# Statistics, small products, weights and score rows re-ordered in the front part of a two-layer attention and expert kernel

## The chip, the core and the metric

The kernel runs on one core of a Trainium2 chip. The metric is the device time of one execution in microseconds. The core has five engines with queues of their own: TensorE (PE; weight loads are listed as PEld), VectorE (DVE), ScalarE (ACT), GpSimd (POOL) and SyncE (SP). SP issues nearly all DMAs; GpSimd issues the gathers and scatters by index.

## What is computed

The reference runs two layers on x and a context, both of 8 x 256 tokens of width 256. Cut to what matters here, the first layer is:

```
q, k, v = norm(x) @ Wq + bq, ctx @ Wq + bq, ctx @ Wq + bq          # 16 columns each
corr    = mean over batch and columns of ifft(fft(q) * conj(fft(k)))  # 256 lags
w, lags = top 12 of corr, softmax of them
x       = x + (sum of w * rolled v, repeated 16 times) @ Wout + bout

norm    = layer_norm(layer_norm(x))
scores  = norm @ centroids.T                                   # 2048 tokens, 8 experts
expert e takes the 256 best tokens not yet taken, in the order of e
x       = x + routed tokens + gelu(norm(routed) @ w1[e] + b1[e]) @ w2[e] + b2[e]
```

The second layer is an attention of 16 heads on the context and a mixture of 8 experts (two of them for each token) with a shared expert. It follows the part that is changed and is not touched.

## The kernel before

All engines' queues are written out by hand (`tc.manual_schedule`): the order of the calls in the code is the order of the instructions on each engine. A queue of small closures, `work`, holds products that can be done at any time (keys and values of the second layer, later the experts' products); `fill(us)` takes from it what is to run on TensorE while VectorE works.

The front part, in the order of time:

- The tokens X and the context C are loaded in four pieces each, transposed to `XT` and `CT`, and the tokens' statistics are taken (`stats_x`). `rstd` (lines 1457 to 1477) makes the inverse deviation of a group: a variance, a power of -0.5 on GpSimd, and, as `newton()`, four small instructions that sharpen it. The result `R1` is spread to `rexp`.
- The correlation goes through DRAM (`Gd`, `DG`), then the softmax weights (`Wd`, `CW`).
- `copy_rows(b)` puts a batch of X into PSUM, `spread_rows` adds the attention's output `PB` to it, `take(bs)` (line 1990) takes each tile's statistics on VectorE (with `raw`, only the raw statistics of one instruction, put together later by `put_together` on GpSimd), copies the tile back to X on ScalarE and stores it to `NMd` in DRAM. For one batch, `act_sums` and `squares` do the statistics on ScalarE.
- `factors(q0, q1, eng)` (line 2039) calls `rstd` for tiles q0 to q1, `widen` (2043) spreads the factors `r2` over 32 columns, `factor_rows(k)` (1950) turns them into rows in PSUM (`psr`), and `times_factors` multiplies the raw scores (`ps0` for expert 0, `psx` for all) by them: `n0` and `SC`. `rows_part` adds a term with `cP`, which comes from the small product `pcp`. `means` writes the second column of the factors, `mr2`; both columns lie in `rm`, and `store_factors` (1936) stores them to `NMd`, beside the rows, in four DMAs.
- `SC` is stored to `SCd` in DRAM, and `load_row(e)` (2161) loads the row of expert e, repeated over the partitions. Zeros are stored to `Yd` and `Od`.
- `search(e, ...)` finds the threshold of expert e in five rounds: VectorE counts (`above`, L2198), TensorE sums the counts (`pcn`, L2215), VectorE moves the threshold. For e > 0 the first instruction (`n`, L2190) needs row e.
- `list_tokens(e, ...)` makes the list of tokens and gathers their rows as R (POOL L2323) from `NMd`. `ffn(e, ids, R)` scales R on ScalarE (L2367), transposes it (`prt`, L2387), and runs the two products with the weights of `load_l0(e)` (1812); `Yd` takes the result by a scatter. The lists of one expert and the products of another run beside the searches.

Tiles come from pools. A pool that is opened after another was closed can lie in the same memory, and then its first writer waits for the last users of the old tiles. `pa` is closed before the searches, and the score rows (pool `prow`) are opened after that; `pr` stays open.

```
    rm = pa.tile([P, NT, 2], F32, name="rm")
...
    nc.sync.dma_start(out=SCd, in_=SC)
    for m in range(2):
        store_factors(m)
    rows = {e: load_row(e) for e in range(1, 3)}
    nc.sync.dma_start(
        out=Yd.rearrange("(c p) d -> p c d", p=P),
        in_=blank[:, 0:D].unsqueeze(1).to_broadcast([P, NT, D]),
    )
    nc.sync.dma_start(out=Od[T:, :], in_=blank[:, 0:D])
    rows.update({e: load_row(e) for e in range(3, E - 1)})
```

Of the kernel before, what the change touches and what calls it, by code (L numbers as in the profile page):

```python
# [9 lines left out]
F32 = mybir.dt.float32  # L10
# [4 lines left out]
ALU = mybir.AluOpType  # L15
# [4 lines left out]
P = 128  # L20
# [1066 lines left out]
def fast_path(  # L1087
# [33 lines left out]
    nc = tc.nc  # L1121
    B, S, D = x.shape
    T = B * S
    NT = T // P
    KC = D // P
    TPB = S // P
    E = L0_ffn_w1.shape[0]
# [6 lines left out]
    NB = D // P  # L1134
# [162 lines left out]
    for dst, src, i in (  # L1297
# [12 lines left out]
        out=WZ[:, :, DH : 2 * DH],  # L1310
# [59 lines left out]
    def column_norms(pn):  # L1370

        for c in range(NB):
            for kc in range(KC):
                nc.tensor.matmul(
                    pn[:, c : c + 1],
                    wsq[:, kc, c * P : (c + 1) * P],
                    ones[:, 0:1],
                    start=(kc == 0),
                    stop=(kc == KC - 1),
                )  # L1380
        nc.scalar.activation(qmax, pn, AF.Copy, scale=257.0)
        nc.gpsimd.tensor_tensor(
            qmax, qmax, powers[:, 1:2].to_broadcast([P, NB]), ALU.pow
        )
        nc.gpsimd.tensor_tensor(qmax, qmax, babs, ALU.add)
# [171 lines left out]
    newton()  # L1557
    newton = stats_x(8, nc.gpsimd)
    turn(X, XT, 8, act, act)
    newton()  # L1560
    newton_l = stats_x(12, nc.gpsimd)
    turn(X, XT, 12, act, act)
    newton()
# [248 lines left out]
    def load_l0(e):  # L1812
        w1 = w0.tile([P, KC, F], F32, tag="w1", name=f"w1_{e}")
        nc.sync.dma_start(out=w1, in_=L0_ffn_w1[e].rearrange("(kc p) f -> p kc f", p=P))
        w2 = w0.tile([P, NF, D], F32, tag="w2", name=f"w2_{e}")
        nc.sync.dma_start(out=w2, in_=L0_ffn_w2[e].rearrange("(fc p) d -> p fc d", p=P))
        return w1, w2

    NMd = dram.tile([T, D + 2], F32, name="NMd")
    Yd = dram.tile([T, D], F32, name="Yd")  # L1820
    Td = dram.tile([E * CAP1 + P, ROW], F32, name="Td")
    Od = dram.tile([T + P, D], F32, name="Od")
    W0 = {0: load_l0(0)}


    order_b = [2 * g + m for m in range(2) for g in range(4)]
# [6 lines left out]
    def copy_rows(b, pool, tag):  # L1833
        pos[b] = pool.tile([P, TPB, D], F32, tag=tag, name="po")
        nc.tensor.matmul(
            pos[b].rearrange("p h d -> p (h d)"),
            ident,
            rows_of(b).rearrange("p h d -> p (h d)"),
            start=True,
            stop=False,  # L1840
            skip_group_check=True,
        )
# [23 lines left out]
    def small_products(j):  # L1866
        for dc in range(KC):
            nc.tensor.matmul(
                pw[:, j, :],
                wrt[:, dc, j * P : (j + 1) * P]  # L1870
                if j < 2
                else boc[:, dc : dc + 1].to_broadcast([P, P]),
                cenP[:, dc, :],
                start=(dc == 0),
                stop=(dc == KC - 1),
            )
# [2 lines left out]
    copy_rows(order_b[1], ps_t, "pt")  # L1879
    small_products(0)  # L1880
    small_products(1)
    copy_rows(order_b[2], ps_t, "pt")
    small_products(2)
    nc.tensor.matmul(pb, ones[:E, :], bdiag, start=True, stop=True)
    column_norms(pw[:, 4, 0:NB])
    nc.vector.tensor_copy(WCn, pw[:, 0:3, :])
    bound = pr.tile([P, E], F32, name="bound")
    nc.vector.tensor_copy(bound, pb)
# [39 lines left out]
    PB = pa.tile([P, D], F32, name="PB")  # L1928
    nc.vector.tensor_tensor(PB, pp, boutb, ALU.add)

    rm = pa.tile([P, NT, 2], F32, name="rm")
    r2, mr2 = rm[:, :, 0], rm[:, :, 1]
    rowv = NMd.rearrange("(c p) d -> p c d", p=P)
    sexp = pa.tile([P, NT, 32], F32, name="sexp")
# [104 lines left out]
    def factors(q0, q1, eng):  # L2039
        qs = slice(q0, q1)  # L2040
        return rstd(MV[:, qs, :], r2[:, qs], 1.0 + LN_EPS, LN_EPS**2, eng, mr2[:, qs])
# [24 lines left out]
    spread_rows(*b[4:6])  # L2066
    squares = act_sums(b[3])
    take(b[:3], True)
    squares()
    pcp = ps_t.tile([P, 32], F32, tag="pt", name="pcp")  # L2070
    for j in range(2):
        nc.tensor.matmul(
            pcp, R3[:, j, :], WCn[:, j, :], start=(j == 0), stop=(j == 1)
        )
    for i in b[6:]:
        copy_rows(i, ps_t, "pt")
    spread_rows(*b[6:])
    cP = pa.tile([P, 32], F32, name="cP")
    nc.vector.tensor_tensor(cP, pcp, WCn[:, 2, :], ALU.add)
    raw_means = put_together(6)  # L2080
    newton_a, means_a = factors(0, 8, nc.gpsimd)

    def rows_part(ps, cols):

        for g in range(4):
# [10 lines left out]
                skip_group_check=True,  # L2096
            )

    rows_part(ps0, cP[:, 0:1].to_broadcast([P, 32]))
    take(b[4:6])  # L2100
    newton_2, means_2 = factors(8, 12, nc.gpsimd)
    rows_part(psx, cP)
    take(b[6:])
    W0[1] = load_l0(1)
    newton_3, means_3 = factors(12, 16, nc.vector)
    newton_a(nc.vector)
    widen(0, 8, nc.scalar)
    factor_rows(0)
    factor_rows(1)
    factors_out(0)  # L2110
    newton_2(nc.vector)
    widen(8, 12, nc.vector)
    factor_rows(2)
    newton_3()
    widen(12, 16, nc.vector)
# [6 lines left out]
    nc.gpsimd.tensor_tensor(SC[:, halves[1]], sx1, srow[:, 1, :], ALU.mult)  # L2122
    raw_means()
    means_a()
    means_2(nc.gpsimd)
    means_3(nc.gpsimd)


# [42 lines left out]
        return row  # L2171

    nc.sync.dma_start(out=SCd, in_=SC)
    for m in range(2):
        store_factors(m)
    rows = {e: load_row(e) for e in range(1, 3)}
    nc.sync.dma_start(
        out=Yd.rearrange("(c p) d -> p c d", p=P),
        in_=blank[:, 0:D].unsqueeze(1).to_broadcast([P, NT, D]),
    )  # L2180
    nc.sync.dma_start(out=Od[T:, :], in_=blank[:, 0:D])
    rows.update({e: load_row(e) for e in range(3, E - 1)})

    def search(e, row, steps, head, each):

# [171 lines left out]

    def ffn(e, ids, R):

        w1, w2 = W0.pop(e)  # L2360
        b2b = pf.tile([P, D], F32, tag="b2b", name="b2b")
        nc.sync.dma_start(out=b2b, in_=L0_ffn_b2[e].partition_broadcast(P))
        RT = pf.tile([P, KC, CAP], F32, tag="RT", name="RT")
        A = pf.tile([P, NF, CAP], F32, tag="A", name="A")
        Y = pf.tile([P, NCT, D], F32, tag="Y", name="Y")
        for r in range(NCT):
            nc.scalar.activation(  # L2367
                R[:, r, 0:D],
                R[:, r, 0:D],
                AF.Identity,  # L2370
                bias=R[:, r, D + 1 :],
                scale=R[:, r, D : D + 1],
            )
            if e in TPART and r == NCT - 1:

                nc.scalar.copy(blank[:, D : D + 1], blank[:, D + 1 : D + 2])
                n0_, n1_ = TPART[e]
                nc.sync.dma_start(
                    out=Td.rearrange("(n p) w -> p n w", p=P)[:, n0_:n1_, :],
                    in_=blank.unsqueeze(1).to_broadcast([P, n1_ - n0_, ROW]),  # L2380
                )

        def turn_rows():
            prt = ps_t.tile([P, KC, NCT, P], F32, tag="pt", name="prt")
            for r in range(NCT):
                for kc in range(KC):
                    nc.tensor.transpose(  # L2387
                        prt[:, kc, r, :], R[:, r, kc * P : (kc + 1) * P], ident
                    )
            for kc in range(KC):  # L2390
                nc.scalar.activation(  # L2391
                    RT[:, kc, :],
                    prt[:, kc].rearrange("p r q -> p (r q)"),
                    AF.Identity,
                    bias=gbc[:, 1, kc : kc + 1],
                    scale=gbc[:, 0, kc : kc + 1],
                )

        work.insert(min(3, len(work)), (0.5, turn_rows))

        def up(f):
            ph = ps_h.tile([P, CAP], F32, tag="ph", name="ph")
            for kc in range(KC):
                nc.tensor.matmul(  # L2404
                    ph,
                    w1[:, kc, f * P : (f + 1) * P],
                    RT[:, kc, :],
                    start=(kc == 0),
                    stop=(kc == KC - 1),
                )  # L2410
                if kc < KC - 1:
                    yield
            nc.scalar.activation(  # L2413
                A[:, f, :], ph, AF.Gelu_apprx_tanh, bias=b1c[:, e, f : f + 1]
            )
            yield

        def down(r):
            py = ps_k.tile([P, D], F32, tag="pm", name="py")
            for f in range(NF):  # L2420
                nc.tensor.matmul(  # L2421
                    py,
                    A[:, f, r * P : (r + 1) * P],
                    w2[:, f, :],
                    start=(f == 0),
                    stop=(f == NF - 1),
                )
                if f < NF - 1:
                    yield
            nc.vector.tensor_tensor(Y[:, r, :], py, b2b, ALU.add)  # L2430
            nc.gpsimd.indirect_dma_start(
                out=Yd,
                out_offset=bass.IndirectOffsetOnAxis(ap=ids[:, r : r + 1], axis=0),
                in_=Y[:, r, :],
                in_offset=None,
            )
            yield

        if e == E - 1:
            work.append((0.0, lambda: first_rows(False)))  # L2440
        for f in range(NF):
            in_steps(up(f), KC)
        if e == E - 1:
            final.append(Y)
            work.append((0.0, lambda: first_rows(True)))
        for r in range(NCT):
            in_steps(down(r), NF)
        if e + 2 < E:
            work.append((0.0, lambda: W0.update({e + 2: load_l0(e + 2)})))

# [1035 lines left out]
```

## Time and profile before

| what | value |
|---|---|
| median of 3 runs | 883.14 us (882.53 to 884.13) |
| the profiled execution | 882.51 us |
| its span in the trace | 880.8 us |
| mean granted clock of TensorE | 0.993 |
| busy TensorE, VectorE, ScalarE, GpSimd | 858.4, 310.0, 266.4, 214.2 us |
| moved by DMA | 105.22 MB |

Durations and moments below are from the profiled execution, and its time is the span and 1.7 us around it. A line of the timeline has start, duration, engine, line of the code, operation, output <- input, sizes, count, and in brackets how long the engine stood idle before it and what ended that. A line of the waits has who waited for whom, the total, how many times, the longest. SPq is SyncE issuing a DMA: its duration is the issuing, not the transfer.

### The profile page before, as it was taken

The numbers are of one execution on the slowest core, as the hardware profiler recorded it, in microseconds if no ns is written. First come the engines' busy times: TensorE is split into PE (matmuls) and PEld (weight loads), VectorE is DVE, ScalarE is ACT, GpSimd is POOL, SyncE is SP. The second block draws the span as 40 slices with busy tenths as digits, with TensorE's granted clock in tenths as the row PEclk, the third lists the DMA queues.
The fourth block names the chain that finished last, engine by engine and source line by source line (L and its number), as shares of the span: only waits on it lengthen the run. The fifth ranks groups of instructions, "written<-read, shape, count | busy, mean of one in ns | idle before, by whom it ended". The sixth has DMA issues, their size and how long they took to land. (4 is left out here: it accounts for less than half of the span.)

```text
span 880.8 us, 11150 instructions
## 1 busy us (share of the span) xinstructions
PE 858.4 (97%) x4180; PEld 535.4 (61%) x4180; DVE 310.0 (35%) x1022; ACT 266.4 (30%) x493; POOL 214.2 (24%) x298
## 2 busy tenths in 40 slices
PE   8988899999999999999999999999999999999997
PEld 6646687778555555545658474747464656474746
DVE  7376877321656665552111212011111111111011
ACT  4243453242577676331010111111111111111110
POOL 7251222211326464323310020111111122111200
PEclk9999999999999999999999999999999999999999
DMA  8474478850420001271210646565647443311130
GB/s 249 156 204 170 155 211 234 257 185 30 129 82 25 2 14 38 77 271 45 71 51 25 192 113 175 155 180 155 180 150 175 158 93 109 89 13 12 14 106 28
DMA packets 87127, 105.22 MB, mean 119 GB/s; under 512 B 8825, under 2 KB 77657, under 8 KB 87033
## 3 DMA queue, kind: packets, MB, share of 16 engines
q1 hardware_dynamic: 78520, 91.10, 32.7%
q0 software_dynamic: 7920, 13.02, 7.1%
q8 instruction: 35, 0.57, 0.3%
q10 hardware_dynamic: 624, 0.30, 0.1%
q14 instruction: 28, 0.22, 0.1%
HBM read 80.60 MB, written 25.37 MB: 120 GB/s over the span
## 5 line engine op out<-in xcount | busy, mean ns | idle before, releaser
L3115 DVE TENSOR_TENSOR A<-A,pu 128x512 f32<-128x512 f32 x96 | 66.0, 688 | 365.1 <-PE pu L3106 358.4
L3114 ACT ACTIVATE A<-pgt 128x512 f32<-128x512 f32 x96 | 57.4, 598 | 271.4 <-PE pgt L3106 271.4
L3175 POOL DMA_INDIRECT Od<-Y,ids x32 | 49.4, 1545 | 302.2 <-ACT Y L3188 207.7
L3106 PE MATMUL pgt<-RT,wa 128*128 128x512 f32 x256 | 121.1, 596 | 0.0
L3106 PE MATMUL pu<-RT,wb 128*128 128x512 f32 x256 | 120.3, 592 | 0.0
L3128 PE MATMUL py<-wc,A 128*128 128x256 f32 x512 | 111.8, 379 | 0.0
L3128 PEld LDWEIGHTS py<-wc,A 128*128 128x128 f32 x512 | 96.7, 190 | 13.3 <-issue 0.5
L3106 PEld LDWEIGHTS pu<-RT,wb 128*128 128x128 f32 x256 | 48.6, 190 | 61.2 <-issue 60.0
L2691 ACT ACTIVATE ex<-p,scale 128x512 f32<-128x512 f32 x128 | 77.3, 690 | 27.5 <-PE p L2683 26.2
L3106 PEld LDWEIGHTS pgt<-RT,wa 128*128 128x128 f32 x256 | 47.6, 190 | 54.9 <-issue 54.5
L2404 PE MATMUL ph<-RT,w 128*128 128x256 f32 x256 | 61.6, 389 | 1.5 <-ACT RT L2391 1.3
L2421 PE MATMUL py<-w,A 128*128 128x256 f32 x256 | 62.0, 389 | 0.0
L2404 PEld LDWEIGHTS ph<-RT,w 128*128 128x128 f32 x256 | 45.3, 190 | 9.9 <-ACT RT L2391 1.8
L2421 PEld LDWEIGHTS py<-w,A 128*128 128x128 f32 x256 | 46.5, 190 | 6.4
L2923 POOL DMA_INDIRECT Td<-HP,to x32 | 31.6, 988 | 65.7 <-DMA Td<-HP,to 62.7
L2413 ACT ACTIVATE A<-ph,b1c 128x256 f32<-128x256 f32 x64 | 30.1, 473 | 54.4 <-PE ph L2404 50.9
L3106 PE MATMUL pgt<-HT,wa_-1_2738 128*128 128x512 f32 x96 | 45.5, 596 | 0.0
L3106 PE MATMUL pu<-HT,wb_-1_2739 128*128 128x512 f32 x96 | 45.1, 592 | 0.0
L3188 ACT ACTIVATE Y<-py,R 128x256 f32<-128x256 f32 x32 | 15.2, 474 | 96.5 <-PE py L3128 96.5
L2683 PE MATMUL p<-QM,KT 32*128 32x512 f32 x256 | 43.4, 640 | 0.4 <-DVE QM L2664 0.4
L3128 PE MATMUL py<-wc_-1_2740,A 128*128 128x256 f32 x192 | 41.9, 379 | 0.0
L3128 PEld LDWEIGHTS py<-wc_-1_2740,A 128*128 128x128 f32 x192 | 36.4, 190 | 5.8 <-issue 1.0
(457 smaller groups left out, 990.6 us busy)
## 6 DMA issues: line engine op xcount, KB each, us to landing
w<-in_L_ffn_w_dram SPq DMA_DIRECT2D x16, 1024.0 KB, 6.9
wa<-in_L_ffn_w_e_dram SPq DMA_DIRECT2D x8, 1024.0 KB, 7.5
wb<-in_L_ffn_w_e_dram SPq DMA_DIRECT2D x8, 1024.0 KB, 8.8
wc<-in_L_ffn_w_e_dram SPq DMA_DIRECT2D x8, 1024.0 KB
R<-Td SPq DMA_DIRECT2D x8, 530.0 KB, 7.0
sa<-in_L_ffn_w_e_dram SPq DMA_DIRECT2D x16, 256.0 KB, 3.9
sb<-in_L_ffn_w_e_dram SPq DMA_DIRECT2D x16, 256.0 KB, 5.1
sc<-in_L_ffn_w_e_dram SPq DMA_DIRECT2D x16, 256.0 KB, 6.5
```

The costliest lines, as they stand in the source:

```text
L2404: nc.tensor.matmul(ph, w1[:, kc, f * P : (f + 1) * P], RT[:, kc, :], start=(kc == 0), stop=(kc == KC - 1),)
L2413: nc.scalar.activation(A[:, f, :], ph, AF.Gelu_apprx_tanh, bias=b1c[:, e, f : f + 1])
L2421: nc.tensor.matmul(py, A[:, f, r * P : (r + 1) * P], w2[:, f, :], start=(f == 0), stop=(f == NF - 1),)
L2683: nc.tensor.matmul(ps[g].rearrange("p m q -> p (m q)"), KT[rows, c, k0 : k0 + P], QM[b][rows, c].rearrange("p m q -> p (m q)"), start=True ...
L2691: nc.scalar.activation(e4[:, g], ps[g], AF.Exp, scale=scale)
L2923: nc.gpsimd.indirect_dma_start(out=Td, out_offset=bass.IndirectOffsetOnAxis(ap=to[g][:, k, j : j + 1], axis=0), in_=HP[:, GT * g + j, :], ...
L3106: nc.tensor.matmul(ps, w_[:, kc, fs], xs[kc], start=(kc == 0), stop=(kc == KC - 1),)
L3114: nc.scalar.activation(a, pgt, AF.Silu)
L3115: nc.vector.tensor_tensor(a, a, pu, ALU.mult)
L3128: nc.tensor.matmul(py, A[:, f, s : s + P], wc[:, f, :], start=(f == 0), stop=(f == NF - 1))
L3175: nc.gpsimd.indirect_dma_start(out=Od, out_offset=bass.IndirectOffsetOnAxis(ap=ids, axis=0), in_=Y, in_offset=None, compute_op=ALU.add,)
L3188: nc.scalar.activation(Y, py, AF.Copy, scale=R[:, i, D + e : D + e + 1])
```

## The change

The four joined parts of it: (1) in the opening, a `newton()` that stood twice for the same group is called once, behind the next group's statistics. (2) The statistics of the layer's second half are put together ahead of ScalarE's squares, the factors are made in groups of 6, 6 and 4 tiles (before: 8, 4, 4), with the first group's Newton steps on GpSimd; the copies of the last two batches go ahead of the small product `pcp`, and `cP` and both `rows_part` go behind the statistics of the batch before the last; `column_norms` goes ahead of a copy and two small products. (3) The weights of expert 1 are loaded right behind those of expert 0, and `b2b`, the bias of the second product, is loaded with the weights instead of in `ffn`. (4) `rm` lies in pool `pr`; rows 1 and 2 are loaded ahead of `store_factors`, and rows 3 to 6 ahead of the zeros of `Yd` and `Od`.

```diff
--- before.py
+++ after.py
@@ -1557,7 +1557,6 @@
     newton()
     newton = stats_x(8, nc.gpsimd)
     turn(X, XT, 8, act, act)
-    newton()
     newton_l = stats_x(12, nc.gpsimd)
     turn(X, XT, 12, act, act)
     newton()
@@ -1814,13 +1813,15 @@
         nc.sync.dma_start(out=w1, in_=L0_ffn_w1[e].rearrange("(kc p) f -> p kc f", p=P))
         w2 = w0.tile([P, NF, D], F32, tag="w2", name=f"w2_{e}")
         nc.sync.dma_start(out=w2, in_=L0_ffn_w2[e].rearrange("(fc p) d -> p fc d", p=P))
-        return w1, w2
+        b2b = w0.tile([P, D], F32, tag="b2b", name=f"b2b_{e}")
+        nc.sync.dma_start(out=b2b, in_=L0_ffn_b2[e].partition_broadcast(P))
+        return w1, w2, b2b
 
     NMd = dram.tile([T, D + 2], F32, name="NMd")
     Yd = dram.tile([T, D], F32, name="Yd")
     Td = dram.tile([E * CAP1 + P, ROW], F32, name="Td")
     Od = dram.tile([T + P, D], F32, name="Od")
-    W0 = {0: load_l0(0)}
+    W0 = {e: load_l0(e) for e in range(2)}
 
 
     order_b = [2 * g + m for m in range(2) for g in range(4)]
@@ -1879,10 +1880,10 @@
     copy_rows(order_b[1], ps_t, "pt")
     small_products(0)
     small_products(1)
+    column_norms(pw[:, 4, 0:NB])
     copy_rows(order_b[2], ps_t, "pt")
     small_products(2)
     nc.tensor.matmul(pb, ones[:E, :], bdiag, start=True, stop=True)
-    column_norms(pw[:, 4, 0:NB])
     nc.vector.tensor_copy(WCn, pw[:, 0:3, :])
     bound = pr.tile([P, E], F32, name="bound")
     nc.vector.tensor_copy(bound, pb)
@@ -1928,7 +1929,7 @@
     PB = pa.tile([P, D], F32, name="PB")
     nc.vector.tensor_tensor(PB, pp, boutb, ALU.add)
 
-    rm = pa.tile([P, NT, 2], F32, name="rm")
+    rm = pr.tile([P, NT, 2], F32, name="rm")
     r2, mr2 = rm[:, :, 0], rm[:, :, 1]
     rowv = NMd.rearrange("(c p) d -> p c d", p=P)
     sexp = pa.tile([P, NT, 32], F32, name="sexp")
@@ -2066,20 +2067,18 @@
     spread_rows(*b[4:6])
     squares = act_sums(b[3])
     take(b[:3], True)
+    raw_means = put_together(6)
+    newton_a, means_a = factors(0, 6, nc.gpsimd)
+    newton_a()
     squares()
+    for i in b[6:]:
+        copy_rows(i, ps_t, "pt")
+    spread_rows(*b[6:])
     pcp = ps_t.tile([P, 32], F32, tag="pt", name="pcp")
     for j in range(2):
         nc.tensor.matmul(
             pcp, R3[:, j, :], WCn[:, j, :], start=(j == 0), stop=(j == 1)
         )
-    for i in b[6:]:
-        copy_rows(i, ps_t, "pt")
-    spread_rows(*b[6:])
-    cP = pa.tile([P, 32], F32, name="cP")
-    nc.vector.tensor_tensor(cP, pcp, WCn[:, 2, :], ALU.add)
-    raw_means = put_together(6)
-    newton_a, means_a = factors(0, 8, nc.gpsimd)
-
     def rows_part(ps, cols):
 
         for g in range(4):
@@ -2096,20 +2095,21 @@
                 skip_group_check=True,
             )
 
+    take(b[4:6])
+    newton_2, means_2 = factors(6, 12, nc.gpsimd)
+    take(b[6:7])
+    cP = pa.tile([P, 32], F32, name="cP")
+    nc.vector.tensor_tensor(cP, pcp, WCn[:, 2, :], ALU.add)
     rows_part(ps0, cP[:, 0:1].to_broadcast([P, 32]))
-    take(b[4:6])
-    newton_2, means_2 = factors(8, 12, nc.gpsimd)
     rows_part(psx, cP)
-    take(b[6:])
-    W0[1] = load_l0(1)
+    widen(0, 6, nc.scalar)
+    take(b[7:])
     newton_3, means_3 = factors(12, 16, nc.vector)
-    newton_a(nc.vector)
-    widen(0, 8, nc.scalar)
+    newton_2(nc.vector)
+    widen(6, 12, nc.scalar)
     factor_rows(0)
     factor_rows(1)
     factors_out(0)
-    newton_2(nc.vector)
-    widen(8, 12, nc.vector)
     factor_rows(2)
     newton_3()
     widen(12, 16, nc.vector)
@@ -2122,7 +2122,7 @@
     nc.gpsimd.tensor_tensor(SC[:, halves[1]], sx1, srow[:, 1, :], ALU.mult)
     raw_means()
     means_a()
-    means_2(nc.gpsimd)
+    means_2()
     means_3(nc.gpsimd)
 
 
@@ -2171,15 +2171,15 @@
         return row
 
     nc.sync.dma_start(out=SCd, in_=SC)
+    rows = {e: load_row(e) for e in range(1, 3)}
     for m in range(2):
         store_factors(m)
-    rows = {e: load_row(e) for e in range(1, 3)}
+    rows.update({e: load_row(e) for e in range(3, E - 1)})
     nc.sync.dma_start(
         out=Yd.rearrange("(c p) d -> p c d", p=P),
         in_=blank[:, 0:D].unsqueeze(1).to_broadcast([P, NT, D]),
     )
     nc.sync.dma_start(out=Od[T:, :], in_=blank[:, 0:D])
-    rows.update({e: load_row(e) for e in range(3, E - 1)})
 
     def search(e, row, steps, head, each):
 
@@ -2357,9 +2357,7 @@
 
     def ffn(e, ids, R):
 
-        w1, w2 = W0.pop(e)
-        b2b = pf.tile([P, D], F32, tag="b2b", name="b2b")
-        nc.sync.dma_start(out=b2b, in_=L0_ffn_b2[e].partition_broadcast(P))
+        w1, w2, b2b = W0.pop(e)
         RT = pf.tile([P, KC, CAP], F32, tag="RT", name="RT")
         A = pf.tile([P, NF, CAP], F32, tag="A", name="A")
         Y = pf.tile([P, NCT, D], F32, tag="Y", name="Y")
```

## Prediction

> **What bounds the kernel now.** I read the page first, then TensorE's waits, then the timeline around the two longest of them, then the granted clock window by window.
>
> ```profile
> span 880.8 us, 11150 instructions
> ...
> PE 858.4 (97%) x4180; PEld 535.4 (61%) x4180; DVE 310.0 (35%) x1022; ACT 266.4 (30%) x493; POOL 214.2 (24%) x298
> ```
>
> TensorE is busy for 858.4 of 880.8 us. From about 108 us on it hardly waits: it works through a fixed queue. So a microsecond that the first 108 us lose or win moves everything behind it by as much. The change touches only this front part, and the question is which of TensorE's waits there it takes away. This is the view of waits, TensorE's own (total, times, longest):
>
> ```profile
> PE prt L2387 <- ACT R L2367: 2.6, 3, 1.2
> PE pcn L2215 <- DVE above L2198: 2.4, 2, 2.2
> ...
> PE psr L1960 <- ACT sexp L2047: 1.8, 1, 1.8
> ...
> PE psr L1960 <- DVE sexp L2049: 0.6, 2, 0.3
> ...
> PE pR L1592 <- POOL rexp L1568: 0.2, 1, 0.2
> ```
>
> Two places matter: 2.2 us before a count matrix (`pcn`) and 1.8 + 0.6 us in the factor stage (`psr`). The timeline of 58 to 84 us shows what stands behind the first (start, duration, engine, line):
>
> ```profile
> 58.72 0.34 SPq L2173 DMA_DIRECT2D SCd<-SC  x1
> 59.84 4.15 SPq L1938 DMA_DIRECT2D NMd<-rm  x4
> 67.46 1.27 SPq L2165 DMA_DIRECT2D row<-SCd  x2
> 68.78 0.47 SPq L2177 DMA_DIRECT2D Yd<-blank  x1
> ...
> 71.24 0.17 DVE L2320 CAST ids<-idf 128x2 uint32<-128x2 f32 x1
> 73.74 0.75 DVE L2190 SCALAR_TENSOR_TENSOR n<-n,lo,row 128x512 f32<-128x512 f32 x1 [2.33 <-DMA row<-SCd]
> ...
> 76.89 5.76 SPq L2165 DMA_DIRECT2D row<-SCd  x4
> ```
>
> VectorE was done with expert 0 at 71.41 and stood 2.33 us until row 1 had landed; TensorE ran dry at 73.11 and stood 2.23 us until the first count of expert 1 (75.34). Row 1 was issued only at 67.46, for two reasons. The SC store before it took 7.8 us to land (66.5), behind the 2 MB of `W0[1]` issued at 54.08. And SP waited 2.9 us more for the four stores of `rm`: `rm` lay in pool `pa`, whose memory the rows take over. Then 2 MB of zeros for `Yd` joined in, and row 1 needed 6.3 us.
>
> The granted clock shows a second price. This is TensorE by windows (span, busy, granted clock, DMA share, GB/s):
>
> ```profile
> 52.35:55.77 3.42, 1.37 (x28) 1.00 0.69 176
> 55.77:59.18 3.41, 3.07 (x15) 0.50 0.83 216
> ...
> 72.83:76.24 3.41, 1.18 (x7) 1.00 1.01 333
> 76.24:79.66 3.42, 3.42 (x11) 0.50 0.43 155
> 79.66:83.07 3.41, 3.41 (x18) 1.00 0.27 98
> 100.13:103.55 3.42, 2.21 (x13) 1.00 0.12 41
> ```
>
> The half clock comes in whole windows of 3.41 us, on one grid (55.77 to 76.24 is six of them), each behind a window in which TensorE was busy for only 1.37 or 1.18 us; 2.21 busy us cost nothing. So the row's wait is paid twice: counts of expert 1 (L2198) begin at 74.53, 76.06, 78.05, 80.55 and 82.08, that is every 1.53 us, but 1.99 and 2.50 us in the half-clock window: 0.46 + 0.97 = 1.43 us more.
>
> **The change, part by part.**
>
> *Rows ahead of factors, `rm` in `pr`, `W0[1]` early.* SC is ready by about 57.9 (factor stage, below). `W0[1]` and two `b2b` (128 KB each) now follow `W0[0]` at 37 us: 37 to 43.5 us moved 2.30 MB at 354 GB/s, so another 2.3 MB end near 50. The eight 256 KB stores of X (issued 46 to 54, at the 1 us pace of ScalarE's copies) queue behind, and by 57 the queue is empty. An SC-sized store on a free queue (Wd, issued 33.62) let the next DMA go at 35.76: 2.1 us. So row 1 is issued near 60.2. Rows 3 to 6 ran alone between 78.5 and 82.5 us at 98 GB/s, with 25% of the engines: 256 KB in 2.6 us, about a microsecond behind the issue. Row 1 lands near 64, against a need at 70.8. Even if SC landed at 66.5 as now, row 1 would be there by 70.1. The stall goes: 2.23 us, and with it the window's 1.43 us. Bounds: 0 (row 1 later than 73.7 less the shift) and 3.66; I take 3.66, since the margin is 6 us.
>
> [...]
>
> *What is late next.* The gather of expert 0's rows R (POOL L2323) stands before the stall and does not move with it. Its second half was issued at 73.86 and took 6.1 to 6.6 us, landing near 80.2; ScalarE used R at 83.01 without a wait. It is now issued 0.6 us earlier and still beside the zeros of `Yd` (behind rows 3 to 6, so from about 71): 79.6. ScalarE will want it at 83.01 - 4.26 = 78.75. TensorE waits 0.85 us in `prt`. Bounds: 0 (the next gathers took 2.9 and 3.6 us) and the slow rival below. The gather also waits for the `rm` stores, now behind rows 1 and 2: their last was issued at 64.0 and SP was let go at 67.46; 2 to 3 us later they still precede 71.7.
>
> *Groups of 6, 6, 4.* GpSimd's chain:
>
> ```profile
> 49.00 0.22 POOL L2033 TENSOR_SCALAR MV<-sums 128x2 f32<-128x2 f32 x1 [2.43 <-ACT sq L2026]
> ...
> 51.01 1.67 POOL L1465 TENSOR_TENSOR x_r<-x_ve,powers 128x8 f32<-128x8 f32 x1
> ...
> 53.04 1.98 POOL L1465 TENSOR_TENSOR x_r<-x_ve,powers 128x4 f32<-128x4 f32 x2
> ```
>
> The joined statistics no longer wait for ScalarE's squares but for VectorE's six raw statistics, done at 47.17. From 47.3: 1.84 us to the power (49.17 to 51.01 now), a power of 6 between 1.01 (width 4) and 1.67 (width 8), 1.34; four Newton steps, now on GpSimd, 1.1; the squares' scaling and the next variance 0.6; power of 6, 1.34; power of 4, 0.99. End 54.55, now 55.02: 0.47 us earlier, and so the third `widen` and the last `psr`. The 1.8 us wait does not go: `cP` now follows `pcp` behind the last spreads (about 51.1), `rows_part` takes 51.1 to 53.1, and the second `widen` (power ends 53.55, VectorE 0.8, ScalarE 0.4) lets `psr` go on at 54.85. The idle time moves, and a half-clock window near 56 stays likely. I take 0.45; bounds -0.6 (VectorE's queue: `cP` waits behind one more tile of statistics, and `rows_part` behind it) and 1.1 (the window stays at full clock: the first `pcn` at 59.51 was 0.65 late for its count).
>
> *Newton steps not run twice.* Four GpSimd instructions of 0.28 us leave the path to `rexp`; TensorE waited only 0.18 us there. I take 0.15; bounds 0 and 0.18.
>
> *Column norms ahead of a copy, `b2b` with the weights.* The eight records of 1.05 us stay in TensorE's queue ahead of `pr3`: 0. That is hidden by TensorE being busy through 38.6; bounds plus and minus 0.2. `b2b` leaves `ffn`, where nobody waited for it: 0; without cover 0.4 us of queue each.
>
> *Sum.* 0.15 + 0.45 + 2.23 + 1.43 - 0.85 = 3.4 us. The profiled execution took 882.51 us (span 880.8), so 879.1; the median of the runs, 883.14, lies 0.63 above it: 879.7.
>
> **Rivals.**
>
> *More than forecast* (R in time, or full clock near 56): 0.85 + 0.65 more, 878.2, at the bounds 877.0. For it: the gathers of 2.9 and 3.6 us. Against: these had no zeros beside them. 0.17.
>
> *The row's wait only changes its name* (R or the `rm` stores become late by most of what is won, so that the change doesn't bring the earlier search it is for): gain 0.6 to 1.5 us, 881.6 to 882.5. For it: R had 2.8 us of slack against 4.26 us of shift. 0.13.
>
> *Slower: R stuck behind the rows.* Four of sixteen engines now carry rows 3 to 6 (1 MB at 98 GB/s, 10.7 us) and their quarter of `Yd` (0.5 MB, 5.2 us) from about 66.5: to 82.4. If the gather's share on them comes last, R lands near 84.4, 5.6 us after 78.75: 1.4 us slower than now, and with one half-clock window 2.8 us: 886. It decides from R landing after 83.0. Against it: gather and zeros shared all engines before and took 6.6 us. [...] 0.10.
>
> *Forecast case*, 878.2 to 881.2: 0.60.
>
> **How the numbers follow.** About 0.2% (1.8 us) is what a measurement of this kernel can tell. Faster than 881.4: forecast 0.60, more 0.17 and a little of the renamed wait, 0.79. Within: 0.11. Slower than 884.9: 0.10. The range leaves out the slow rival and half of the far end on the fast side: 877.0 to 882.2.
>
> **What would show it.** Right: no VectorE idle before L2190 for expert 1, no half-clock window behind it, row 1 issued by 61, SC landing in about 2 us, last `psr` some 0.6 us earlier. Wrong: row 1 issued after 66; `prt` of expert 0 waiting over 2 us for R; a new half-clock window between 60 and 100.

## The result, and the profile after

| | median of its executions | from, to | executions |
|---|---|---|---|
| before | 882.72 us | 881.38, 884.84 | 12 |
| changed | 882.80 us | 878.60, 884.99 | 12 |

The ratio is 0.9994, with an interval of [0.9974, 1.0013]; a second comparison on another chip gave 883.23 against 883.95 us, 0.9994 [0.9982, 1.0006]. So no gain is clear of noise (0.5 us by the ratio, and at most 2.3 us by the wider interval). The forecast was 3.4 us less.

The profiled execution alone would have told another story. It took 878.66 us, where the sum gave 879.1 (page of the changed kernel; span, then busy time):

```profile
span 876.9 us, 11147 instructions
...
PE 856.0 (98%) x4180; PEld 533.7 (61%) x4180; DVE 308.8 (35%) x1017; ACT 266.2 (30%) x494; POOL 213.8 (24%) x298
```

Its waits of TensorE between 30 and 120 us are close to the forecast: the 2.2 us before the count are gone, the waits before `psr` are smaller (0.7 and 0.2 us; 0.8 us went to `ps`, which waits for `cP`), and R costs 1.0 us where 0.85 was reckoned:

```profile
...
PE prt L2385 <- ACT R L2365: 1.0, 2, 0.5
PE ps L2086 <- DVE cP L2102: 0.8, 1, 0.8
PE psr L1961 <- ACT sexp L2048: 0.7, 1, 0.7
PE pcn L2215 <- DVE above L2198: 0.2, 1, 0.2
PE psr L1961 <- DVE sexp L2050: 0.2, 1, 0.2
```

And these are lines of its timeline (start, duration, engine, line; SPq is SyncE issuing a DMA):

```profile
60.77 1.27 SPq L2165 DMA_DIRECT2D row<-SCd  x2
62.13 4.76 SPq L1939 DMA_DIRECT2D NMd<-rm  x4
...
69.23 0.17 DVE L2320 CAST ids<-idf 128x2 uint32<-128x2 f32 x1
69.61 0.75 DVE L2190 SCALAR_TENSOR_TENSOR n<-n,lo,row 128x512 f32<-128x512 f32 x1 [0.20 <-DMA NMd<-rm]
...
71.96 1.24 POOL L2323 DMA_INDIRECT R<-NMd,ids  x1 [6.71 <-PE pp L1412]
...
78.70 0.60 ACT L2365 ACTIVATE R<-R 128x256 f32<-128x256 f32 x1 [1.34 <-DMA R<-NMd,ids]
```

One gap in it had no place in the sum: the list of expert 0 (`ids`) is done at 69.40, and the gather that uses it starts at 71.96. In the kernel before it started 1.08 us after `ids` began (71.24, 72.32); here 2.73. This is the line of the kernel before:

```profile
72.32 1.24 POOL L2323 DMA_INDIRECT R<-NMd,ids  x1 [5.84 <-PE pp L1412]
```

In this comparison the times of the changed kernel spread more than those before (in the second one they did not: 881.5 to 887.0 us against 880.7 to 886.6). Five executions from 878.6 to 881.4 us had a mean granted clock of 0.997, seven from 882.3 to 885.0 had 0.992 to 0.995. By estimate (half of 3.41 us in a span of 877 us) one window of 3.41 us at half clock takes 0.2% from the mean, so the upper group had one to three windows more. A trace of such an execution (886.96 us, on the second chip) shows this:

```profile
61.90 1.27 SPq L2165 DMA_DIRECT2D row<-SCd  x2
63.27 4.52 SPq L1939 DMA_DIRECT2D NMd<-rm  x4
...
67.95 0.17 DVE L2320 CAST ids<-idf 128x2 uint32<-128x2 f32 x1
...
73.24 1.24 POOL L2323 DMA_INDIRECT R<-NMd,ids  x1 [9.27 <-DVE w L2205]
...
79.65 0.60 ACT L2365 ACTIVATE R<-R 128x256 f32<-128x256 f32 x1 [3.58 <-DMA R<-NMd,ids]
...
80.31 0.44 PE L2385 MATMUL prt<-ident,R 128*128 128x128 f32 x2 [2.68 <-ACT R L2365]
```

The search was 1.3 us earlier than in the first trace (`ids` at 67.95), the gather 1.3 us later (73.24). TensorE stood 2.68 us, and 0.95 us more before the second half of R. Its windows (span, busy, granted clock, DMA share, GB/s) show what followed:

```profile
78.71:82.12 3.41, 0.87 (x4) 0.99 0.98 355
82.12:85.53 3.41, 2.75 (x8) 0.50 0.37 132
85.53:88.95 3.42, 3.42 (x13) 0.51 0.27 97
...
102.60:106.01 3.41, 1.38 (x23) 0.99 0.52 155
106.01:109.42 3.41, 3.41 (x10) 0.51 0.71 237
```

Behind the wait for R came two half-clock windows, 82.12 to 88.95 (0.50 and 0.51); two more came at 106.01 and 167.45 (0.51 each).

### The profile page after: what moved, and what is told of

It reads as the page before. It is cut to its first block, busy times and chain, and to the rows that moved or that the text cites. A ratio compares the mean times of both kernels' runs of the same rounds, so it can differ in the third digit from the quotient of the medians.

```text
span 876.9 us, 11147 instructions
## 1 busy us (share of the span) xinstructions
PE 856.0 (98%) x4180; PEld 533.7 (61%) x4180; DVE 308.8 (35%) x1017; ACT 266.2 (30%) x494; POOL 213.8 (24%) x298
## 5 line engine op out<-in xcount | busy, mean ns | idle before, releaser
L3112 ACT ACTIVATE A<-pgt 128x512 f32<-128x512 f32 x96 | 57.3, 597 | 271.5 <-PE pgt L3104 271.5
```

The lines of the kernel that those rows point to most:

```text
L3112: nc.scalar.activation(a, pgt, AF.Silu)
```

## The experiments

Two theories came first: that the half-clock windows merely fall elsewhere in some executions (1), and that a transfer is late (2); a third, that another part of the change costs what the rows win (3). After the first four runs there was a new one, **the gate**: the gather of R cannot start before the four stores of `rm` have landed, and the change put these behind rows 1 and 2, which wait until SC has landed. Each comparison is with the kernel before, run on the same chip; the chips differ by some 2 us, so ratios are compared. Where the expectations say "2.3 us after ids", they count from an earlier cast of the list (L2308); the table below counts from the last one (L2320), from which it is 1.1.

| run | median, us | before, us | ratio, interval |
|---|---|---|---|
| rows_only | 880.35 | 881.85 | 0.9990 [0.9977, 1.0003] |
| rows_undone | 879.15 | 881.85 | 0.9980 [0.9969, 0.9990] |
| norms_back | 882.60 | 881.85 | 1.0010 [0.9992, 1.0028] |
| after_third (changed) | 883.23 | 883.95 | 0.9994 [0.9982, 1.0006] |
| stores_first | 878.47 | 883.95 | 0.9953 [0.9933, 0.9972] |
| zeros_first | 885.90 | 883.95 | 1.0020 [1.0003, 1.0037] |
| weights_late | 887.10 | 883.95 | 1.0044 [1.0025, 1.0064] |
| stores_first_2 | 877.63 | 881.60 | 0.9961 [0.9944, 0.9978] |
| rows_undone_2 | 879.35 | 881.60 | 0.9982 [0.9970, 0.9993] |
| before_stores_first | 878.32 | 881.60 | 0.9967 [0.9957, 0.9978] |
| stores_filled | 879.14 | 881.60 | 0.9978 [0.9968, 0.9989] |

**after_look**: no edit.

> The changed kernel once more, unaltered, for the trace of another execution. Its 12 timed executions lay in two groups: 878.6 to 881.4 us with a granted clock of 0.997, and 882.3 to 885.0 with 0.992 to 0.995; the profile at hand is of the first group. Theory 1 (windows at other places): the steps of the change are as in that profile (row 1 issued near 60.8, no wait before L2190 for expert 1), and a time above 882 comes with two or three more half-clock windows of 3.41 us, each worth 1.2 to 1.7 us, at other stages than behind expert 1's row. Theory 2 (a late transfer): a time above 882 comes with a longer wait of TensorE for R (prt waits over 3.7 us in all) or for a row, and the windows lie behind it. If the time is below 881, the trace shows one or no window in the first 110 us and tells nothing between the two.

879.57 us, one window at 81.89 and none before. `ids` at 67.80, gather at 71.89, `prt` waited 2.9 us. With no window ahead of it the search was 1.43 us earlier than in the first trace (67.80 against 69.23), and the gather only 0.07. What the search won, the wait for R took. By what was expected ahead of it, a time below 881 us could not decide between the two theories; but a gather that stays where it was pointed at a late transfer, and set the question what holds it.

**rows_only**: the kernel before with parts 3 and 4.

```diff
-    W0 = {0: load_l0(0)}
+    W0 = {e: load_l0(e) for e in range(2)}
...
-    rm = pa.tile([P, NT, 2], F32, name="rm")
+    rm = pr.tile([P, NT, 2], F32, name="rm")
...
+    rows = {e: load_row(e) for e in range(1, 3)}
     for m in range(2):
         store_factors(m)
-    rows = {e: load_row(e) for e in range(1, 3)}
+    rows.update({e: load_row(e) for e in range(3, E - 1)})
```

> The kernel before with parts 3 and 4 of the change alone: early weights, rm in pr, rows ahead of the factors' stores and of the zeros. Theory 1: the wait of 2.23 us before expert 1 goes here too, so the median is 1.5 to 3.5 us below the kernel before, or the executions spread in two groups like the changed kernel's (877 to 881 and 882 to 885) with the mean granted clock. Theory 2 (late transfer): same as before within 1 us, with R or a row late. Theory 3 (another part of the change costs what the rows win): 879 to 880.5 us in the median, all executions well below the kernel before, since the costly part is not in it.

The interval holds 1. The wait before expert 1 did go (`n` waited 0.56 us), but the gather came 2.38 us after `ids`.

**rows_undone**: the changed kernel with those lines put back; the groups and products stay.

> The changed kernel without parts 3 and 4: old place of the second weights, rm in pa, rows behind the factors' stores and the zeros; new groups, norms and products stay. Theory 1: the wait of 2.2 us before expert 1 is back; the median lies 0 to 1 us from the kernel before (gain of 0.6 us from the groups at most), and its lowest execution is not below 880.5. Theory 3: 884 to 886 us, slower than before by what the other parts cost (1.5 to 3 us), with a new wait or new windows in the first 58 us.

This was the surprise: faster than before, where no more than 0.6 us was given it, and with its row still late (1.96 us before `n`). Theory 3 falls: the parts other than the rows don't cost, they gain. The changed kernel's ratio was 0.9994 in both its comparisons; which speaks for parts 3 and 4, as they stand, taking that gain away (the intervals of the two still overlap).

**norms_back**: the column norms behind the third copy again.

```diff
     small_products(1)
-    column_norms(pw[:, 4, 0:NB])
     copy_rows(order_b[2], ps_t, "pt")
     small_products(2)
     nc.tensor.matmul(pb, ones[:E, :], bdiag, start=True, stop=True)
+    column_norms(pw[:, 4, 0:NB])
```

> The changed kernel with the eight products of the column norms behind the third copy and the last small products, as before. They are 8 products of one column, some 1 us in TensorE's queue, in a stretch that the half clock follows. Theory 1: the same two groups as the changed kernel, median 880 to 883.5. Theory 3, if the longer stretch of small products is what draws the windows: no execution above 882, median 879 to 880.

877.2 to 885.3 us, spread like the changed kernel in its first comparison: nothing shows that the place of these eight products matters.

**after_third** is the execution shown above.

> The changed kernel unaltered, on one chip beside the three that follow, and for the trace of one more execution. New theory (stores gate the gather): the gather of R cannot start before the four stores of rm have landed, and these now stand behind rows 1 and 2, which wait for SC to land; the gather starts near 71.9 whatever the search has done (71.96 and 71.89 in the two traces, 3.9 and 5.3 us after ids, against 2.3 us in the kernel before). Then the same two groups again, median 881 to 883.5; and in a trace of a time above 882 the gather starts at 71.5 to 73, prt waits 1 to 4 us, and two or three half-clock windows lie elsewhere. Rival (windows alone, no gate): a slow trace with no more than 1 us of wait in prt.

**stores_first**: one pair of statements of the changed kernel exchanged.

```diff
     nc.sync.dma_start(out=SCd, in_=SC)
-    rows = {e: load_row(e) for e in range(1, 3)}
     for m in range(2):
         store_factors(m)
+    rows = {e: load_row(e) for e in range(1, 3)}
     rows.update({e: load_row(e) for e in range(3, E - 1)})
```

> The changed kernel with one pair of lines exchanged: the four stores of rm ahead of rows 1 and 2, everything else as in it. Theory (stores gate the gather): the stores are issued from about 59 and land before 67, so the gather follows ids by 2.3 us, near 69 to 70.5, R is used without more than 0.5 us of wait, row 1 is issued by 64 and still in time; median 876.5 to 879, no group above 881.5. Rival (the half-clock windows fall elsewhere for any reason, the gate does not matter): the same two groups as the changed kernel, median 880.5 to 883.5. Second rival (row 1 late again): a wait of 0.5 to 2 us before L2190 of expert 1 and 879 to 881.

0.9953 [0.9933, 0.9972], and 0.9961 [0.9944, 0.9978] the second time (stores_first_2). Its timeline:

```profile
57.49 2.43 SPq L1939 DMA_DIRECT2D NMd<-rm  x4
61.99 8.43 SPq L2165 DMA_DIRECT2D row<-SCd  x6
...
67.79 0.17 DVE L2320 CAST ids<-idf 128x2 uint32<-128x2 f32 x1
...
68.45 0.75 DVE L2190 SCALAR_TENSOR_TENSOR n<-n,lo,row 128x512 f32<-128x512 f32 x1 [0.48 <-DMA row<-SCd]
68.88 1.43 POOL L2323 DMA_INDIRECT R<-NMd,ids  x1 [5.07 <-PE pp L1412]
...
77.60 0.60 PE L2385 MATMUL prt<-ident,R 128*128 128x128 f32 x4
```

The stores now use the time in which SP waited for SC to land anyway. Row 1 is issued 0.1 us later than in the trace of 886.96 us (61.99, 61.90) and costs `n` 0.48 us; the gather starts 1.09 us after `ids`; `prt` has no idle time in brackets. Nothing else was moved, so the gate is shown by this exchange. On this chip it was worth 4.8 us in the median (883.23 to 878.47); by the ratios of the two runs 2.9 and 3.6 us.

**zeros_first**: rows 3 to 6 behind the zeros again.

> The changed kernel with rows 3 to 6 behind the zeros of Yd and Od, as before. It tells whether R is late because of what shares the DMA engines with it: the rows on four engines (rival of the prediction) or the gate of the rm stores. Theory of the gate: the gather starts near 72 all the same and the times stay in the two groups, median 880.5 to 883.5. Rival (rows on four engines hold R back): R lands 1.5 to 3 us earlier after its issue, median 878 to 880.

2.7 us slower than the changed kernel on the same chip, by the medians; the two intervals overlap slightly. The gather started at 73.00, held as before, but R was used 8.35 us after that (81.35), against 6.41 in the trace of 886.96 us. So having rows 3 to 6 between the stores and the zeros did not delay R; with the 2 MB of zeros there, R came later.

**weights_late**: the changed kernel, expert 1's weights at their old place.

> The changed kernel with the weights of expert 1 (2.3 MB) loaded at their old place, about 54 us, so that SC's store queues behind them again. Theory of the gate: SC lands near 64 to 66, so rows 1 and 2, the rm stores and the gather each come 3 to 5 us later than in the changed kernel: gather at 75 to 77, prt waits 4 to 7 us, median 884 to 888. Rival (windows alone): as the changed kernel within 1.5 us.

Gather at 75.45, as expected; `prt` waited 3.6 us, row 1's count 2.3 us. The dose answers: SC late, so rows, stores and gather late.

The gate in ten traces (us; the first column is the end of SP's issuing):

| trace | last `rm` store issued | `ids` | gather | gather after `ids` | after the stores |
|---|---|---|---|---|---|
| before | 63.99 | 71.24 | 72.32 | 1.08 | 8.33 |
| rows_undone | 62.10 | 69.36 | 70.44 | 1.08 | 8.34 |
| stores_first | 59.92 | 67.79 | 68.88 | 1.09 | 8.96 |
| rows_only | 67.81 | 70.58 | 72.96 | 2.38 | 5.15 |
| changed, 878.66 us | 66.89 | 69.23 | 71.96 | 2.73 | 5.07 |
| norms_back | 67.27 | 68.41 | 72.58 | 4.17 | 5.31 |
| after_look | 66.34 | 67.80 | 71.89 | 4.09 | 5.55 |
| zeros_first | 67.50 | 67.77 | 73.00 | 5.23 | 5.50 |
| after_third | 67.79 | 67.95 | 73.24 | 5.29 | 5.45 |
| weights_late | 70.10 | 67.94 | 75.45 | 7.51 | 5.35 |

In the first three the gather follows `ids` by 1.1 us whatever the stores did (so too in the four runs below); in the other seven it follows the stores by 5.1 to 5.6 us whatever `ids` did.

**stores_first_2, rows_undone_2, before_stores_first**: the same two versions on one chip, and the kernel before with parts 3 and 4 and the exchange, without the groups.

> The version with the stores of rm ahead of rows 1 and 2 once more, on one chip beside the next three, for its size. It was 0.9953 of the kernel before [0.9933, 0.9972]. Theory (stores gate the gather): 0.994 to 0.997 of the kernel before again, the gather 2.3 us behind ids, prt without a wait over 0.5 us. Rival (the first result was a lucky spread of half-clock windows): 0.998 to 1.001.

> The changed kernel without parts 3 and 4, beside the version with the stores first, to size what early rows are worth once the gather is not held. Its trace had the row's wait of 1.9 us with no half-clock window behind it. Theory: 1.5 to 3 us slower than the version with the stores first, 0.997 to 0.999 of the kernel before. Rival (rows are worth nothing, only the other parts gain): within 0.7 us of it.

> The kernel before with parts 3 and 4 and the stores of rm left ahead of the rows: no new groups, no moved products. It tells the rows' part from the groups' part. Theory (gains add up: rows 2.2 us of wait and part of a window, groups 0.5 to 1 us and the smaller wait in psr): 0.9965 to 0.9985 of the kernel before, 0.5 to 2 us slower than the version with everything. Rival (the groups do nothing): equal to the version with everything within 0.5 us.

Groups and products alone gain 2.25 us (881.60 to 879.35), rows with the stores first 3.28 (to 878.32), both 3.97 (to 877.63). They don't add up, and 0.7 us between the last two is less than the intervals can tell apart. rows_undone_2 has a row wait about as long as the kernel before's, 2.11 against 2.23 us on TensorE, but no half clock behind it:

```profile
71.74 0.19 PE L2214 MATMUL pcn<-B32h,cnt 128*128 128x32 f16 x1 [2.11 <-DVE above L2197]
...
66.80:70.21 3.41, 2.83 (x14) 1.00 1.06 355
70.21:73.62 3.41, 1.88 (x10) 1.00 0.97 324
73.62:77.03 3.41, 3.41 (x17) 1.00 0.28 99
```

The grid of the windows (fixed by a window at 100.92, nine windows on) cuts this wait into 0.6 and 1.5 us. In the kernel before, the same wait (73.11 to 75.34) lay wholly inside one window (72.83 to 76.24), with 1.18 us of work and a clock of 0.50 behind it.

**stores_filled**: two steps of keys into the waits of the factor stage.

```diff
+    fill(0.43)
     rows_part(ps0, cP[:, 0:1].to_broadcast([P, 32]))
...
+    fill(0.43)
     factor_rows(1)
     factors_out(0)
```

> The version with the stores first and two steps of the second layer's keys (0.51 us of TensorE each) put into TensorE's two waits of the factor stage (before rows_part and before the second pair of factor rows). If TensorE's amount of work sets the time: 0.8 to 1.1 us less than the version with the stores first, and fewer windows near 55. If the chain factors, search, ids, gather, R sets it (as the gate theory says: R was used at 76.23 right as TensorE came to it at 77.60): TensorE runs out of filling 1 us earlier, prt waits 0.5 to 1.2 us more, and the time is the same within 0.7 us, or up to 2 us more if that wait draws a half-clock window.

A median of 1.5 us more than stores_first_2, with intervals that overlap; in no case the 0.8 to 1.1 us less that more work in the waits could have brought. In its trace the wait before `ps` fell from 0.8 to 0.3 us and that before `psr` for ScalarE went, but the work was missing later: `pid` waited 0.5 us more, `pcn` 0.6, `prt` 0.3, and behind a window with only 1.13 us of work (94.43 to 97.84) came two at half clock (0.50 and 0.52). No execution had a clock above 0.996; three of seven had 0.999 without the filling. Work moved into one wait opened another.

## Why the prediction was wrong

- **The row's wait.** Right as a step: row 1 was issued at 60.8 and 61.9 (forecast 60.2), `n` waited 0.20 us instead of 2.33. The way there was not: SC's store was to meet an empty queue and let row 1 go 2.1 us later. It was issued at 57.35, 55.92 and 56.08 in the three traces of the changed kernel, and row 1 followed after 3.4, 4.6 and 5.8 us; in the first one the DMA engines were still fully busy from 56 to 57.3 us and to 0.81 until 58.5. So SC was ready early and landed late, and whatever stood behind rows 1 and 2 got nothing of the gain. (The 2.9 us that SP "waited more" for the stores in the kernel before lay almost wholly within the wait for SC: the stores let it go at 66.9 to 67.5, SC landed at 66.5.)
- **The window behind it, 1.43 us.** Right for the trace, wrong as a fixed price. rows_undone_2 had nearly the same wait and paid nothing. The term is a chance times a price, and the sum of the trace before took the whole of it.
- **R, 0.85 us.** This is the step that failed, in its sentence on the stores: "2 to 3 us later they still precede 71.7". That they would be issued 2 to 3 us later was about right (last one at 66.9, 66.3 and 67.8 instead of 64.0). Two things were wrong. Their release was read as 67.46, when SP was let go, 3.5 us after the last issue; behind the rows the gather started only 5.1 to 5.6 us after it, at 71.9 to 73.2. (Some 0.9 us of that may be the gather's own start, which it takes after the end of `ids` where nothing holds it.) And 71.7 was a need shifted by only 0.6 us, and taken from an execution with two half-clock windows ahead of the search (38.71 and 55.78). In the first trace after, with one of them, `ids` came 2.0 us earlier, and the gather was wanted at 70.3. With none, the list is done another 1.4 us earlier, and the gather is wanted at 68.9. A fixed moment was set against a moving one: the wait grows with all that is won ahead of it, so windows spared there, and the groups' gain, were given back at `prt`: 1.0, 2.9 and 3.6 us in the three traces. That the first of them met the forecast's 0.85 us, and its time to 0.5 us, was luck.
- **A new window between 60 and 100** was named as what would prove it wrong. Two came in the trace of 886.96 us, behind the wait at `prt`, and one in after_look. The trace of 886.96 us against stores_first on the same chip: 885.2 and 875.1 us of span. The first count of expert 2 begins at 77.55 and 77.69, the fourth `above` after it at 94.35 and 87.48, so 7.0 us are lost between: 3.63 of waits and two windows at a clock of 0.50 and 0.51, by estimate up to 1.7 us each (half of 3.41). Two windows behind that (0.51 each) make another 3.4: 10.4 against a difference of 10.1.
- **Groups, 0.45 us.** Mis-sized: parts 1 and 2 together, 0.60 in the sum, measured 2.25 us in rows_undone_2, by the interval 0.6 to 2.6. The last `psr` came 0.98 us earlier instead of 0.47 (55.15, 56.13). TensorE's waits in this stage fell from 2.4 to 1.7 us, in smaller pieces, and no trace with the new groups had a window between 50 and 60 us, while two of the three with the old ones had. That the missing window makes up the rest is likely, but no run separates it.
- **Newton, column norms, `b2b`.** Put at 0.15, 0 and 0. norms_back does not speak against the second; `pR` no longer waits its 0.2 us. The rest is below what these runs can tell.
- **The rivals.** "The row's wait only changes its name" was the right one and named the stores; it was priced with R alone and without the windows behind R, and left 0.6 to 1.5 us of gain (measured 0.5 us, with intervals that don't exclude this). "R stuck behind the rows" on four engines fell: R was used 6.7 and 6.4 us after the gather's start in two traces after, at 78.7 and 79.7 us, well ahead of the 83.0 that was to decide it, and it was worse with the zeros ahead of it (8.35).

What stays open: the other two windows of the trace of 886.96 us (106 and 167 us) follow waits that the change did not bring, of 1.4 us in every trace before `pid` (1.9 in stores_filled) and for a later R (between 120 and 200 us, 2.6 us in all in the kernel before and 2.7 in the first trace after). Why the changed kernel met them more often than the kernel before in the first comparison was not tried. Why SC landed later than reckoned was not tried either.

## What to carry to other kernels

When a step is moved ahead in a queue, write down for each step it passes who waits for that step and how long before its need it lands, with the need shifted by all that the change wins; what passes for slack in a trace may be a delay that the change itself removes. Here four stores of 4 KB behind two waiting row loads undid some 3 to 5 us, and ahead of them they cost the row 0.5 us in one trace and nothing in the other. And compare spreads, not one profile: the changed kernel's first trace agreed with a wrong forecast to 0.5 us.

## What the runs showed of the hardware

In these traces the length of the idle gap alone did not tell where the half clock came. In the kernel before, the 2.23 us before expert 1's count lay in one window of 3.41 us with 1.18 us of work, and the next window had a clock of 0.50. The 2.11 us of rows_undone_2 lay in two windows with 2.83 and 1.88 us of work, and the window behind them had 1.00.

Twelve traces show half-clock windows. Their time from 28 to 200 us was laid out along the grid that these windows give. Of 17 windows of 3.41 us in which TensorE was busy for 0.75 to 1.72 us, 16 were followed by one at half clock (0.50 to 0.58; not so 1.11 us, weights_late, 68.70, followed by 1.00). Between 1.77 and 1.87 us one of four was (1.85 us, weights_late, 181.34, followed by 0.55). From 1.94 us on, none was, but for two kinds: two windows that were at half clock themselves (2.53 us, stores_filled, and 2.76 us, after_third, followed by 0.52 and 0.51), and those around 35 to 38 us in three traces (before, after, rows_undone, followed by 0.51, 0.54 and 0.51), which are busy for 3.27 to 3.41 us by the records, more than half of it with products of 1 to 32 columns (34.77 to 38.18 in the first trace after: 0.97 and 0.53 us with 32 columns, 1.03 with one, 0.39 with 8). These are counts over twelve traces of one kernel and its variants; what sets the clock was not shown.

The grid lay at different places in three traces of the changed kernel. The first half-clock window begins at 38.18, 81.89 and 82.12 us; thirteen windows on from 38.18 is 82.55. Each window at half clock costs, by estimate, up to 1.7 us (half of 3.41).
